# A decoder with ternary weights on one core: the sums of the weights' magnitudes go to ScalarE, and gate and up are rounded one stage earlier and kept in memory

## The chip, the cores and the metric

The kernel runs on one NeuronCore of a Trainium2 chip. Five engines work side by side, each through its own queue of instructions in order: TensorE (PE in the profile, its weight loads PEld), VectorE (DVE), ScalarE (ACT), GpSimd (POOL) and SyncE (SP), which here issues nearly all DMA transfers. They wait for each other through semaphores. The metric is device time in microseconds (us) of one execution; a run's time is 1607.21 us in the median of three (1605.46 to 1613.25).

## The reference

A decoder of two layers works on `x` of 4 x 512 x 512 in float32. Each layer has self-attention, cross attention to a context and a feed-forward network, each followed by an addition and a layer norm. The change lies in the weights of layer 0's feed-forward, whose three matrices (gate and up, 2048 x 512, and down, 512 x 2048) are made ternary:

```python
scale = 1.0 / jnp.clip(jnp.mean(jnp.abs(w)), EPS)
wq = jnp.clip(jnp.round(w * scale), -1.0, 1.0) / scale
```

and then used in

```python
gate = bitlinear(x, w_gate)
up = bitlinear(x, w_up)
intermediate = jax.nn.silu(gate) * up
return h_bitlinear(intermediate, w_down)
```

So the mean magnitude of a whole matrix must be known before its first element can be rounded: each matrix is read twice, once for the mean and once for rounding.

## The kernel before

**Tiling.** Everything is cut into tiles of 128 partitions x 512 columns (256 KB in float32). One of the four batches of one phase is a Python generator; the phases are A (self-attention), B (cross attention), C (feed-forward) of layer 0 and D, E, F of layer 1. `lanes` runs two generators at a time in turn, so the end of one batch overlaps the start of the next, and also the end of A3 with the start of B0. Beside them `step` advances background generators once a round, as `BESIDE` lists: `C0` from A1 to A3, and `C` from B0 to B2.

**The background work before.** `l0_ffn_scales` (`C0`, lines 541 to 571) goes over the 16 chunks of each of the three matrices in the order gate, up, down. It loads a chunk into one of four `w` buffers and VectorE sums its magnitudes into one column (`TENSOR_REDUCE`, L556). After 16 chunks VectorE adds up the columns (L564), a one-column matmul adds over the partitions (`tot`, L567), and VectorE makes mean and scale (L569, L570). `l0_ffn_weights` (`C`, lines 573 to 603) loads all 48 chunks again into the same four buffers. VectorE rounds each by two instructions (L585: times the scale plus a magic number, so that the float's own rounding does it; L586: clipping), and ScalarE casts it to bf16 (L594) into half of a tile of the pool `o`, where it stays until the feed-forward uses it. That pool of 69 buffers also holds the operands of the attention phases.

**The attention phases.** In A, TensorE works in float32 split into a high and a low part: `split` lets ScalarE cast the high part (L141) and VectorE or GpSimd subtract for the low part (L144). Queries and keys go PSUM, ScalarE (L338), VectorE (times sine, L347), GpSimd (times cosine, L350; sum, L355), `split`. GpSimd also adds the bias to `x` (L406) and makes the low part of the next batch's input `xTl` (L144). The softmax takes its maximum on VectorE (L396) and its exponential on ScalarE (L398). In B, one step of the inner loop handles a pair of heads and 128 queries: six score matmuls (L524), maxima on VectorE (L472), exponentials on ScalarE (L474), normalizing on GpSimd (L480), eight transposes on TensorE (L246), copies from PSUM on ScalarE and VectorE (L487), and the output matmuls (L496). There are 64 such steps.

**What sets the order.** A scheduler of the framework orders the instructions of each engine at build time by priorities in program order, data dependencies and free buffers. `issue_after` adds a wish to it: an instruction is queued on its engine behind a named one. `self.mark` names the last multiplication by the sine on VectorE, and the sums of L556 are queued behind it. A `Pipe` delays a step by a number of rounds, so that a load has time to land before its consumer is queued.

## Time and profile before

| What | us |
|---|---|
| Median of the runs, and their range | 1607.21 (1605.46 to 1613.25) |
| The profiled execution's own time | 1603.95 |
| Its span, first to last instruction | 1602.1 |
| Self-attention of layer 0, about | 40 to 245 |
| Cross attention of layer 0, about | 242 to 447 |
| First and last sum of magnitudes (L556) | 48.6 and 227.7 |
| First and last rounding (L585, L586) | 229.0 and 408.0 |
| Last cast to bf16 (L594) | 523.2 |

The page says how busy each engine is; a share over the whole span mixes stages with different limits, so the stages are read one by one, as the busy time of each engine in windows of the span. A row of a tile gives the shortest, median and longest duration of its instructions, and when the first and last of them started. A row of waits gives who waited for whom, the total in us, how often, and the longest.

### The profile page before, as it was taken

How to read it: one execution, taken by the hardware profiler on the slowest of the kernel's cores; microseconds unless marked ns; L12 is line 12 of the kernel's file. 1: busy time of each engine (PE TensorE's matmuls, PEld its weight loads, DVE VectorE, ACT ScalarE, POOL GpSimd, SP SyncE). 2: the span in 40 equal slices, each digit the busy share in tenths (PEclk: the TensorE clock that was granted, in tenths of full speed). 3: DMA queues.
4: the chain of work that ended last, by engine and by line, in shares of the span. 5: the costliest groups of instructions: out<-in, count | busy, mean ns of one | idle time of the engine just before them, and what ended most of it. 6: DMA issues, size and time to landing. Idle time of an engine off the chain costs nothing.

```text
span 1602.1 us, 25568 instructions
## 1 busy us (share of the span) xinstructions
PE 1522.8 (95%) x8246; PEld 1094.9 (68%) x8246; DVE 1237.3 (77%) x2676; ACT 1015.7 (63%) x2193; POOL 666.6 (42%) x672
## 2 busy tenths in 40 slices
PE   8999999999999999999999999999998889999995
PEld 6888785444544674477777767777676766787874
DVE  6486589999876788877575665756869899888896
ACT  5333337988778887787796756968633444645552
POOL 6664654555535204422334242343423345334342
PEclk9999999999999999999999999999999999999998
DMA  7053444455125634852523323233444532020101
GB/s 252 29 171 105 130 161 134 135 171 178 54 79 153 214 108 139 273 175 68 142 58 78 80 87 115 64 80 80 159 158 141 181 100 66 10 80 1 54 0 53
DMA packets 127812, 180.76 MB, mean 113 GB/s; under 512 B 16560, under 2 KB 51376, under 8 KB 127680
## 3 DMA queue, kind: packets, MB, share of 16 engines
q1 hardware_dynamic: 123552, 170.69, 33.9%
q0 software_dynamic: 4128, 8.46, 2.1%
q8 instruction: 65, 1.06, 0.3%
q14 instruction: 67, 0.55, 0.1%
HBM read 111.98 MB, written 41.94 MB: 96 GB/s over the span
## 4 chain that ended last, share of the span: by engine, by line
PE 59%; DVE 19%; ACT 8%; issue 5%; DMA 4%; POOL 3%; SPq 1%; DVEq 0%; ACTq 0%; POOLq 0%
PE fg L1159 7%; PE facc L1142 5%; PE dT L925 3%; DVE bsm L472 3%; PE dn L739 2%; DVE fg L1115 2%; ACT de L915 2%; PE do L945 2%; PE qk L154 2%; PE qk L153 2%; PE qk L152 2%; PE had L753 2%; PE pu L687 2%; PE bo L496 2%; PE pg L685 2%
## 5 line engine op out<-in xcount | busy, mean ns | idle before, releaser
L1115 DVE SCALAR_TENSOR_TENSOR fg<-fg,gs,fg 128x512 f32<-128x512 f32 x220 | 162.2, 743 | 24.6 <-ACT fg L1107 16.2
L911 DVE CUSTOM_DVE_ANT_0 de<-ds,negm,thr 128x128 f32<-128x128 f32 (+3 forms) x256 | 126.4, 545 | 34.6 <-PE ds L900 28.0
L915 ACT ACTIVATE de<-de,dm 128x128 f32<-128x128 f32 (+3 forms) x256 | 143.1, 563 | 12.4 <-DVE dm L911 11.9
L1159 PE MATMUL fg<-fxh,gu 128*128 128x512 f32 x352 | 141.6, 402 | 6.3 <-DVE fg L1115 3.2
L480 POOL TENSOR_SCALAR be<-be,bsm 128x512 f32<-128x512 f32 x128 | 96.1, 764 | 103.0 <-DVE bsm L478 65.5
L1159 PE MATMUL fg<-fxl,gu 128*128 128x512 f32 x352 | 137.5, 391 | 0.0
L662 POOL TENSOR_TENSOR hl<-g,hh 128x512 fp32r<-128x512 f32 x64 | 83.6, 1313 | 109.4 <-ACT hh L661 90.3
L1119 POOL TENSOR_TENSOR fg<-fg,fg 128x512 f32<-128x512 f32 x44 | 60.9, 1384 | 133.0 <-DVE fg L1115 51.9
L474 ACT ACTIVATE be<-bs,bsm 128x512 f32<-128x512 f32 x128 | 87.3, 690 | 30.9 <-DVE bsm L472 28.9
L842 POOL TENSOR_TENSOR dql<-dqf,dqh 128x512 fp32r<-128x512 f32 x32 | 41.3, 1290 | 155.3 <-ACT dqh L841 121.1
L925 PE MATMUL dT<-ident,de 128*128 128x128 f32 x640 | 89.6, 278 | 7.6 <-ACT de L915 5.8
L1159 PEld LDWEIGHTS fg<-fxh,gu 128*128 128x128 f32 x352 | 66.0, 187 | 34.2 <-DVE fg L1115 13.9
L925 PEld LDWEIGHTS dT<-ident,de 128*128 128x128 f32 x640 | 71.7, 141 | 25.3 <-ACT de L915 13.6
L472 DVE TENSOR_REDUCE bsm<-bs 128x1 f32<-128x512 f32 x128 | 83.3, 671 | 0.0
L496 PE MATMUL bo<-bpT,cT 128*64 128x512 f32 x256 | 76.4, 618 | 2.1 <-ACT bpT L487 1.2
L246 PEld LDWEIGHTS bT<-ident,be 128*128 128x128 f32 x512 | 55.0, 141 | 34.2 <-issue 12.3
L246 PE MATMUL bT<-ident,be 128*128 128x128 f32 x512 | 73.3, 281 | 3.7 <-POOL be L480 2.1
L1159 PEld LDWEIGHTS fg<-fxl,gu 128*128 128x128 f32 x352 | 66.1, 188 | 12.0
L350 POOL TENSOR_TENSOR z<-z,rope_cos 128x512 f32<-128x512 f32 x32 | 46.7, 1473 | 64.8 <-DVE zs L347 57.7
L1107 ACT ACTIVATE fg<-fg,gs 128x512 f32<-128x512 f32 x88 | 60.1, 683 | 20.3 <-PE fg L1159 20.3
L1142 PE MATMUL facc<-p4h,fhh 128*128 128x512 f32 x176 | 69.9, 398 | 3.2 <-ACT fg L1111 1.5
L685 PE MATMUL pg<-qT,tb 128*128 128x512 bf16 x256 | 66.8, 381 | 4.4 <-ACT qT L647 2.8
(342 smaller groups left out, 4644.9 us busy)
## 6 DMA issues: line engine op xcount, KB each, us to landing
x<-x SPq DMA_DIRECT2D x176, 256.0 KB, 3.0
had_scratch<-hw SPq DMA_DIRECT2D x64, 256.0 KB, 2.3
z<-had_scratch SPq DMA_DIRECT2D x64, 256.0 KB, 5.8
stk<-dqh SPq DMA_DIRECT2D x192, 64.0 KB, 2.0
tw<-in_wg_t SPq DMA_DIRECT2D x32, 256.0 KB, 3.6
tw<-in_wu_t SPq DMA_DIRECT2D x32, 256.0 KB, 3.7
tw<-in_wd_t SPq DMA_DIRECT2D x32, 256.0 KB, 2.8
p<-in_gu_p SPq DMA_DIRECT2D x22, 256.0 KB, 2.8
```

What stands on the lines that cost most here:

```text
L246: self.nc.tensor.transpose(pt[:, i * P : (i + 1) * P], srcs[i][:, j * P : (j + 1) * P], self.ident)
L472: nc.vector.tensor_reduce(sm[:, h : h + 1], ps, AX.X, ALU.max, negate=True)
L474: nc.scalar.activation(e, ps, AF.Exp, bias=sm[:, h : h + 1], accum_out=sm[:, 2 + h : 3 + h])
L480: nc.gpsimd.tensor_scalar(es[h][i], es[h][i], sm[:, 4 + h : 5 + h], 1.0, ALU.mult, ALU.mult)
L496: nc.tensor.matmul(po[0][h * 64 : h * 64 + 64, :], cT[j][:, c : c + 64], pTs[h], start=j == 0, stop=j == NT - 1)
L685: nc.tensor.matmul(pg, tern["wg_t"][k, c][:, m], qT[k], start=k == 0, stop=k == NT - 1)
L911: nc.vector.tensor_tensor_reduce(es[i], ps, self.negm[:, 384 - P * i :], -1.0, self.thr[:, i : i + 1], ALU.add, ALU.min, n4[:, i : i + 1])
L915: nc.scalar.activation(es[i], es[i], AF.Exp, bias=n4[:, i : i + 1], scale=-1.0, accum_out=den[:, hh * 4 + i : hh * 4 + i + 1])
L925: nc.tensor.transpose(pt[:, o + (i - j) * P : o + (i - j + 1) * P], es[i][:, j * P : (j + 1) * P], self.ident)
L1115: self.emitted["DVE"] = nc.vector.scalar_tensor_tensor(y[u], ps, s, y[u], ALU.mult, ALU.add)
L1142: nc.tensor.matmul(acc[t], h[l][:, c], self.dn[i][r], start=i == 0 and n == 0, stop=i == 10 and n == 2)
L1159: nc.tensor.matmul(ps, self.gu[i, u][:, g * P : (g + 1) * P], xT[g][n], start=n == 0, stop=n == 1)
```

## The change

ScalarE, not VectorE, sums the magnitudes: an Abs with an accumulated sum, queued behind the last evacuation of queries and keys (`self.turned`, recorded in `evac`). The background generator of the self-attention, now `l0_ffn_ternary`, does two things in each of its 48 rounds: it loads a chunk of the matrix whose mean it is taking, and, from the second matrix on, it loads a chunk of the matrix before it into a buffer of `o` (`tq`), rounds it on VectorE, casts it on ScalarE into half of a bf16 tile (`tb`), and stores each full tile to DRAM (`tern_kept`, 8 tiles of 256 KB for each of gate and up). So gate is rounded while up is summed, and up while down is summed. In the cross attention `l0_ffn_weights` rounds the 16 chunks of down alone and, beside them, loads the 16 kept tiles of gate and up back into `o`, one of each in three rounds.

```diff
+        self.tern_kept = {name: scratch(name + "_kept", (8, P, 512)) for name in self.TERNARY[:2]}
...
-            nc.scalar.activation(z, ps, AF.Identity, bias=..., scale=...)
+            self.turned = nc.scalar.activation(z, ps, AF.Identity, bias=..., scale=...)
...
+    def ternary(self, pipe, name, done):
+        nc = self.nc
+        cur = []
+
+        def quant(n, f):
+            with self.tc.issue_after(self.mark.ins):
+                nc.vector.tensor_scalar(f, f, self.scale[name], MAGIC, ALU.mult, ALU.add)
+            nc.vector.tensor_scalar(f, f, MAGIC + 1.0, MAGIC - 1.0, ALU.min, ALU.max)
+            pipe.later(1, put, n, f)
+
+        def put(n, f):
+            if n % 2 == 0:
+                cur.append(self.o("tb", BF16, 1024))
+            o = cur[0]
+            with self.tc.issue_after(self.turned.ins):
+                nc.scalar.activation(o[:, n % 2 * 512 : n % 2 * 512 + 512], f, AF.Copy, bias=-MAGIC)
+            if n % 2:
+                cur.clear()
+                done(n // 2, o)
+
+        return quant
...
-            def absum(f, n):
-                with self.tc.issue_after(self.mark.ins):
-                    nc.vector.tensor_reduce(part[:, n : n + 1], f, AX.X, ALU.add, apply_absolute_value=True)
+        def absum(f, part, n):
+            with self.tc.issue_after(self.turned.ins):
+                nc.scalar.activation(f, f, AF.Abs, accum_out=part[:, n : n + 1])
+
+        def keep(name, n, o):
+            pipe.later(1, lambda: nc.sync.dma_start(self.tern_kept[name][n], o.bitcast(F32)))
+
+        old = None
+        for new in self.TERNARY:
+            chunks = self.ternary_chunks(new)
+            part = self.c(new + "_abs", [P, len(chunks)])
+            if old:
+                quant = self.ternary(pipe, old, lambda n, o, name=old: keep(name, n, o))
+                todo = self.ternary_chunks(old)
+            for n in range(len(chunks)):
+                pipe.tick()
+                pipe.later(1, absum, self.load(self.w("tw"), chunks[n][2]), part, n)
+                if old:
+                    pipe.later(2, quant, n, self.load(self.o("tq"), todo[n][2]))
+                yield
...
+        order = [(name, n) for c in range(0, 8, 2) for name in self.TERNARY[:2] for n in (c, c + 1)]
+        quant = self.ternary(pipe, "wd_t", lambda n, o: use("wd_t", n, o))
+        for n, (name, m) in enumerate(order):
+            pipe.tick()
+            pipe.later(1, quant, n, self.load(self.w("tw"), self.ternary_chunks("wd_t")[n][2]))
+            yield
+            pipe.tick()
+            o = self.o("tb", BF16, 1024)
+            self.load(o.bitcast(F32), self.tern_kept[name][m])
+            use(name, m, o)
+            yield
             yield
```

More of the change, by code (lines that the diff above doesn't have):

```diff
@@ L337, in evac @@
             z = zs[w, m] = self.t("z")
-            nc.scalar.activation(z, ps, AF.Identity, bias=self.qkb[:, w * NT + m : w * NT + m + 1], scale=1.0 if w else P ** -0.5)
+            self.turned = nc.scalar.activation(z, ps, AF.Identity, bias=self.qkb[:, w * NT + m : w * NT + m + 1], scale=1.0 if w else P ** -0.5)
             if m % 2:
@@ L539, in ternary_chunks, with l0_ffn_ternary @@
         return [(k, c, w[k * P : (k + 1) * P, c * 512 : (c + 1) * 512]) for c in range(w.shape[1] // 512) for k in range(w.shape[0] // P)]
-    def l0_ffn_scales(self):
+    def ternary(self, pipe, name, done):
[16 more added lines that the diff above has]
+        return quant
+    def l0_ffn_ternary(self):
         nc = self.nc
@@ L549, in l0_ffn_scales @@
         pipe.later(3, nc.vector.tensor_copy, self.had, f[:, 0:P])
-        for name in self.TERNARY:
-            chunks = self.ternary_chunks(name)
-            part = self.c(name + "_abs", [P, len(chunks)])
-            def absum(f, n):
-                with self.tc.issue_after(self.mark.ins):
-                    nc.vector.tensor_reduce(part[:, n : n + 1], f, AX.X, ALU.add, apply_absolute_value=True)
-            for n, (k, c, ap) in enumerate(chunks):
+        def absum(f, part, n):
[11 more added lines that the diff above has]
+            for n in range(len(chunks)):
                 pipe.tick()
-                pipe.later(1, absum, self.load(self.w("tw"), ap), n)
+                pipe.later(1, absum, self.load(self.w("tw"), chunks[n][2]), part, n)
+                if old:
+                    pipe.later(2, quant, n, self.load(self.o("tq"), todo[n][2]))
                 yield
-            yield from pipe.drain()
-            m = self.c(name + "_mean", [P, 4])
+            pipe.tick()
+            m = self.c(new + "_mean", [P, 4])
             nc.vector.tensor_reduce(m[:, 2:3], part, AX.X, ALU.add)
             yield
+            pipe.tick()
             ps = self.pb("tot")
@@ L568, in l0_ffn_scales, with use @@
             yield
+            pipe.tick()
             nc.vector.tensor_scalar(m[:, 0:1], ps[:, 0:1], 1.0 / (len(chunks) * P * 512), 1e-5, ALU.mult, ALU.max)
             nc.vector.reciprocal(m[:, 1:2], m[:, 0:1])
-            self.mean[name], self.scale[name] = m[:, 0:1], m[:, 1:2]
+            self.mean[new], self.scale[new] = m[:, 0:1], m[:, 1:2]
+            old = new
+        yield from pipe.drain()
     def l0_ffn_weights(self):
-        nc = self.nc
         yield from self.bg["C0"]
         pipe = Pipe()
-        order = [("wg_t", x) for x in self.ternary_chunks("wg_t")]
-        up = [("wu_t", x) for x in self.ternary_chunks("wu_t")]
-        order = [e for c in range(4) for e in order[4 * c : 4 * c + 4] + up[4 * c : 4 * c + 4]]
-        order += [("wd_t", x) for x in self.ternary_chunks("wd_t")]
-        cur = []
-        def quant(name, k, c, f):
-            nc.vector.tensor_scalar(f, f, self.scale[name], MAGIC, ALU.mult, ALU.add)
-            nc.vector.tensor_scalar(f, f, MAGIC + 1.0, MAGIC - 1.0, ALU.min, ALU.max)
-            pipe.later(1, put, name, k, c, f)
-        def put(name, k, c, f):
-            if not cur:
-                cur.append(self.o("tb", BF16, 1024))
-            o = cur[0][:, 0:512] if len(cur) == 1 else cur[0][:, 512:1024]
-            cur.append(o)
-            nc.scalar.activation(o, f, AF.Copy, bias=-MAGIC)
-            self.tern[name][k, c] = o
-            if len(cur) == 3:
-                cur.clear()
-        for name, (k, c, ap) in order:
-            pipe.tick()
-            pipe.later(1, quant, name, k, c, self.load(self.w("tw"), ap))
+        def use(name, n, o):
+            for h in range(2):
+                k, c, _ = self.ternary_chunks(name)[2 * n + h]
+                self.tern[name][k, c] = o[:, h * 512 : h * 512 + 512]
+        order = [(name, n) for c in range(0, 8, 2) for name in self.TERNARY[:2] for n in (c, c + 1)]
+        quant = self.ternary(pipe, "wd_t", lambda n, o: use("wd_t", n, o))
+        for n, (name, m) in enumerate(order):
+            pipe.tick()
+            pipe.later(1, quant, n, self.load(self.w("tw"), self.ternary_chunks("wd_t")[n][2]))
+            yield
+            pipe.tick()
+            o = self.o("tb", BF16, 1024)
+            self.load(o.bitcast(F32), self.tern_kept[name][m])
+            use(name, m, o)
+            yield
             yield
@@ L1240, in body @@
             net.l0_attn_weights()
-        net.bg = {("B", 0): net.l0_xattn_ctx(0), "C0": net.l0_ffn_scales(), "C": net.l0_ffn_weights(), "D": net.l1_attn_weights(), "F": net.l1_ffn_weights()}
+        net.bg = {("B", 0): net.l0_xattn_ctx(0), "C0": net.l0_ffn_ternary(), "C": net.l0_ffn_weights(), "D": net.l1_attn_weights(), "F": net.l1_ffn_weights()}
         f = [net.l0_attn, net.l0_xattn, net.l0_ffn, net.l1_attn, net.l1_xattn, net.l1_ffn]
```

## The prediction

> **What bounds the kernel now.** I read the page first, then the busy time of each engine by stage, then single tiles. The span is 1602.1 us; the profiled execution took 1603.95 us, 3.3 us less than the median of the runs shown (1607.21 us).

> ```profile
> PE 1522.8 (95%) x8246; PEld 1094.9 (68%) x8246; DVE 1237.3 (77%) x2676; ACT 1015.7 (63%) x2193; POOL 666.6 (42%) x672
> ```

> TensorE (PE) is busy nearly always, so the question is where it is held up. The change touches two stages: the self-attention of layer 0 (about 40 to 245 us) and its cross attention (about 242 to 447 us). The busy time by stage of the cross attention (columns: window, its length, busy us of PE, PEld, DVE, ACT, POOL with counts, clock, DMA share, GB/s):

> ```profile
> 280.00:320.00 40.00, 38.51 (x220) 19.05 (x216) 38.62 (x87) 36.51 (x91) 22.44 (x28) 1.00 0.43 139
> 320.00:360.00 40.00, 39.05 (x224) 19.71 (x222) 39.51 (x84) 35.63 (x87) 23.28 (x29) 1.00 0.55 171
> 360.00:400.00 40.00, 38.16 (x223) 19.58 (x222) 39.65 (x89) 35.62 (x87) 23.19 (x30) 1.00 0.54 177
> 400.00:440.00 40.00, 39.45 (x239) 20.48 (x238) 35.10 (x79) 31.09 (x79) 20.92 (x29) 1.00 0.16 56
> ```

> VectorE (DVE) is full up to 400 us, and TensorE gets through 220 to 224 matmuls; in the last window, where the rounding of weights runs out at 408 us, it gets through 239. The timeline of TensorE there shows the undisturbed step of the loop, and the row of its score matmuls the whole stage:

> ```profile
> 423.69 0.50 PE L524 MATMUL bs<-kh,qh 64*128 64x512 f32 x2
> 426.62 0.50 PE L524 MATMUL bs<-kh,qh 64*128 64x512 f32 x2
> 429.54 0.49 PE L524 MATMUL bs<-kh,qh 64*128 64x512 f32 x2
> ```

> ```profile
> L524 PE MATMUL bs<-kh,qh x128: 492/494/502, 241.7 to 444.2; 64*128 64x512 f32 x128
> ```

> One step is 2.92 us undisturbed; the 64 steps start between 241.7 and about 444 us, 3.21 us apart on average. 63 x (3.21 - 2.92) = 18.3 us are lost in this stage. Who causes it, from the waits between 262 and 398 us: VectorE, directly and through ScalarE (ACT) and GpSimd (POOL).

> ```profile
> POOL be L480 <- DVE bsm L478: 28.7, 22, 2.2
> ACT be L474 <- DVE bsm L472: 14.0, 22, 1.7
> PEld bo L496 <- DVE bpT L487: 5.2, 10, 1.2
> ```

> The self-attention is the opposite: TensorE is full, VectorE mostly is not, ScalarE is a third busy. Its last part, cut at the hand-over to the cross attention:

> ```profile
> 160.00:200.00 40.00, 38.25 (x168) 30.35 (x167) 21.40 (x34) 13.97 (x27) 25.82 (x20) 1.00 0.41 129
> 200.00:226.00 26.00, 26.00 (x122) 21.60 (x121) 23.46 (x35) 9.65 (x18) 22.23 (x17) 1.00 0.50 167
> 226.00:246.00 20.00, 19.66 (x99) 15.81 (x99) 18.03 (x41) 7.89 (x19) 0.43 (x1) 1.00 0.49 158
> ```

> **The change, part by part.** The rows of the moved work:

> ```profile
> L586 DVE TENSOR_SCALAR tw<-tw x48: 383/416/1374, 230.0 to 408.0; 128x512 f32<-128x512 f32 x48
> L556 DVE TENSOR_REDUCE wd_t_abs<-tw x16: 658/670/687, 195.8 to 227.7; 128x1 f32<-128x512 f32 x16
> L585 DVE TENSOR_SCALAR tw<-tw,wg_t_mean x16: 465/478/910, 229.0 to 333.0; 128x512 f32<-128x512 f32 x16
> ```

> Neighbours overlap by some 80 ns in these rows, so I count by starts: a sum of magnitudes 0.60 us, the pair that rounds one chunk 0.40 + 0.33 = 0.73 us, the cast on ScalarE (median 626 ns) 0.53 us.

> 1. Cross attention, VectorE. Of 48 pairs, 44 ran here; 16 stay. 28 x 0.73 = 20.4 us leave a stage in which VectorE was full. Load left: the window 400 to 440 held 35.1 us, 2.5 us of it rounding, so 32.6 of 40 (82%) without any; one pair in three steps adds 0.24 per 2.92 us (8%). At 90% VectorE no longer paces TensorE; late next is a short burst (normalizing the previous batch). The undisturbed last batch shows what remains: 15 steps took 45.6 us, 1.8 us over the floor. I take 1.5 us a batch, 6 us in all: gain 18.3 - 6 = 12 us. Bounds: 15 (only the four bursts of about 0.85 us remain) and 7 (twice the residue).

> 2. Cross attention, ScalarE and DMA. 44 casts become 16, which frees 15 us (28 x 0.53) of an engine at 36 of 40; it hides behind VectorE and is in the same gain. 44 loads become 16 loads of the down weights plus 16 of kept bf16 pairs, on SP's queue; nobody needs a kept pair before the feed-forward, over 100 us later for most. The last four casts, at 523 us, leave the feed-forward, where TensorE shows no stall next to them: 0 (bounds 0 and -1.5, the one stall of that batch at 556 us).

> 3. Self-attention, ScalarE. 48 Abs with an accumulated sum: nearest row, Square with accumulation at L1172, 622 ns plus a 192 ns read, 0.6 to 0.7 us by starts, so 29 to 34 us; plus 32 casts, 17 us. Some 48 us on an engine with about 70 us of work in 200 us: it reaches 60%, but an evacuation or cast can now stand behind one sum and one cast (1.1 us). The program gains no load of ScalarE's function table.

> 4. Self-attention, VectorE. 48 sums (28.8 us) leave, 32 - 4 more pairs come (20.4 us): less in total. But they behave differently beside GpSimd. The sums' rows stay within 658 to 687 ns though GpSimd ran at the start of 42 of 48. The second rounding instruction has a median of 0.41 us with GpSimd idle at its start, 0.84 with GpSimd running, at most 1.37; the rope multiply on VectorE (L347) reaches 1.81 from 0.68, and GpSimd's own instructions stretch from 1.28 to 1.82.

> That hits the place where TensorE has no slack, the start of the last batch, where GpSimd works without a break (its timeline):

> ```profile
> 165.60 6.21 POOL L406 TENSOR_TENSOR x<-x,bvo 128x512 f32<-128x512 f32 x4
> 171.77 4.99 POOL L144 TENSOR_TENSOR xTl<-xT,xTh 128x512 fp32r<-128x512 f32 x4
> ```

> TensorE waits 2.5 us there (173 to 177 us). In the new order of VectorE seven rounding instructions lie beside this chain where sums lay; at 0.35 us each they push it by 2.5 us, and the late evacuation ahead of it by 1 us: 3.5 us of stall. Bounds: 0 (each slips into a gap) and 6 (a whole 0.8 us each).

> 5. The hand-over. In the new order 6.2 us of rounding for the up weights lie between 226 and 246 us, where 3.5 us lay; VectorE has about 2 us idle in those 20 us. The softmax of the last batch and the first query tiles stand in the same queue, and TensorE's transposes there started 0.05 us after their ScalarE input. I take 2.5 us; bounds 0 and 6.

> 6. DMA and SP's queue. The transfers of these weights in the self-attention rise from 52 to 96 (256 KB each), 16 of them stores, and each store waits for its second cast with the next loads behind it. In the busiest stretch (215 to 225 us) the queue moved 278 GB/s at a DMA share of 0.85; the new average from 104 us on is about 127 transfers in 141 us, 236 GB/s. It fits, with longer landings; the bound above is in the rival. 0 taken. TensorE's order is unchanged but for the three one-column matmuls of the means, each placed up to 11 us earlier, with the sums then 8 us done.

> [...]

> **Sum.** -12 + 3.5 + 2.5 = -6 us: 1598 us for a profiled execution, 1601 us beside the median of 1607.

> **Rivals.**
> - The self-attention swallows everything, as 40% idle engines suggest; the stalls of steps 4 and 5 stay out. -12 to -14 us: 1594 us. For it: total VectorE work there falls by 8 us. Against it: the zero slack at 173 and 239 us.
> - Both ends cancel: steps 4 and 5 at their upper bounds, 12 - 12: 1607 us.
> - Slower: SP's queue becomes the limit of the self-attention. A store of a kept pair waits for ScalarE, the next load of weights for sums waits behind the store, and ScalarE waits in order for that load with TensorE's evacuations behind it. With 16 stores, 1.6 us exposed at each gives 26 us in place of steps 4 and 5, less 12: 1621 us. It decides from 1.3 us a store. Landings of 3 to 6 us speak for it, four load buffers and the shallow load before 200 us against it.

> That the work is not moved is excluded: VectorE's program is 48 instructions shorter, ScalarE's 48 longer, SP's 32 longer.

> **How the numbers follow.** Forecast 0.41 (own range 1596 to 1606), swallowed 0.25, cancelled 0.18, slower 0.16. What a measurement can tell from no change is 0.5%, 8 us. Faster than 1599.2: all but a little of the second case and 0.12 of the first, 0.36. Slower than 1615: 0.15. Between: 0.49. The range runs from the low end of the second case, 1592, to the cancelled case with the spread of the runs, 1612.

> **What would show it.** Right: the steps of the cross attention near 2.95 us, VectorE at about 36 of 40 there, the first score matmul of the cross attention some 6 us later than 241.7, a longer TensorE stall at 173 us, rounding instructions of 0.8 us and more before 226 us. Wrong: ScalarE or VectorE waiting on DMA of weights for more than 10 us before 245 us (slower), or the cross attention starting on time (faster).

## The result and the profile after

The changed kernel takes 1615.86 us (median of 6 runs, 1613.08 to 1618.94) against 1607.01 us before (6 runs): a ratio of 1.005, 95% interval 1.0036 to 1.0064. It is slower by 9 us; forecast was a gain of 6. Its profiled execution took 1617.94 us, 14.0 us more than that of before; 5 us of this are the draw of the two profiled executions.

The first line of the page shows little:

```profile
PE 1526.5 (94%) x8246; PEld 1100.6 (68%) x8246; DVE 1239.8 (77%) x2628; ACT 1046.7 (65%) x2289; POOL 671.4 (42%) x672
```

The row of the score matmuls cuts the loss in two:

```profile
L525 PE MATMUL bs<-kh,qh x128: 492/494/625, 258.7 to 452.3; 64*128 64x512 f32 x128
```

Before, these ran from 241.7 to 444.2 us. The cross attention starts 17.0 us later and takes 193.6 us instead of 202.5, so it gains 8.9 us. Set against each other matmul by matmul, TensorE is 7.4 us late after 185 us, 14.9 after 232, 17 to 18 at the hand-over, 8.3 at the end of the cross attention, 11.3 from 570 us on, and 13.7 at the end.

The busy time of the cross attention, same stretches and columns as before:

```profile
280.00:320.00 40.00, 39.11 (x233) 19.85 (x232) 36.77 (x80) 35.01 (x88) 25.27 (x30) 1.00 0.44 146
320.00:360.00 40.00, 39.39 (x243) 20.74 (x242) 34.46 (x73) 33.33 (x84) 23.90 (x30) 1.00 0.45 145
360.00:400.00 40.00, 38.93 (x227) 19.58 (x226) 34.18 (x75) 33.23 (x84) 22.96 (x32) 1.00 0.40 132
400.00:440.00 40.00, 40.00 (x250) 21.08 (x246) 32.88 (x72) 33.85 (x86) 22.97 (x31) 1.00 0.28 94
```

VectorE is down from 39 of 40 us to 34 to 37 up to 400 us, and TensorE up to 227 to 250 matmuls. But between 262 and 398 us ScalarE waits longer for VectorE's maxima than the 14.0 us of before:

```profile
ACT be L475 <- DVE bsm L473: 22.7, 28, 2.4
```

The self-attention is where the time went. Stretches of 20 us from 160 us on (window, length, busy us of PE, PEld, DVE, ACT, POOL with counts, granted clock, DMA share, GB/s), and what TensorE waited for between 100 and 262 us, where before it waited only 1.7 us for GpSimd and 0.3 for ScalarE:

```profile
160.00:180.00 20.00, 13.15 (x53) 10.12 (x52) 20.00 (x20) 10.21 (x24) 17.40 (x12) 0.84 0.52 152
180.00:200.00 20.00, 20.00 (x82) 16.33 (x81) 11.09 (x22) 10.19 (x24) 5.78 (x4) 0.90 0.85 285
200.00:220.00 20.00, 20.00 (x97) 16.54 (x97) 19.11 (x22) 12.64 (x28) 13.29 (x9) 1.00 0.52 155
220.00:240.00 20.00, 14.87 (x57) 11.48 (x56) 19.93 (x29) 14.18 (x36) 16.12 (x11) 0.83 0.77 248
```

```profile
PE as L154 <- DVE qkl L145: 6.8, 2, 6.5
PE pv L155 <- DVE apl L145: 3.8, 1, 3.8
PE bs L525 <- ACT qh L468: 2.2, 1, 2.2
PE pv L153 <- ACT aph L142: 1.3, 1, 1.3
```

In the first stretch VectorE is busy for all 20.00 us and gets through 20 instructions, one a microsecond. The timeline at 170 to 178 us shows why (start, us, engine, what, and in brackets what ended the idle time):

```profile
169.79 2.88 POOL L407 TENSOR_TENSOR x<-x,bvo 128x512 f32<-128x512 f32 x2
...
171.48 2.88 DVE L234 TENSOR_SCALAR x<-x,ln 128x512 f32<-128x512 f32 x2
172.63 5.92 POOL L145 TENSOR_TENSOR xTl<-xT,xTh 128x512 fp32r<-128x512 f32 x4
...
174.28 1.48 DVE L550 TENSOR_SCALAR tq<-tq,wg_t_mean 128x512 f32<-128x512 f32 x1
...
175.68 1.75 DVE L145 TENSOR_TENSOR qkl<-z,qkh 128x512 fp32r<-128x512 f32 x1
...
177.35 1.49 DVE L551 TENSOR_SCALAR tq<-tq 128x512 f32<-128x512 f32 x1
...
177.48 0.80 PE L154 MATMUL as<-qkl,qkh 128*128 128x512 f32 x1 [6.48 <-DVE qkl L145]
```

VectorE and GpSimd take turns. Each rounding instruction and each normalization (x<-x,ln, 0.54 us when alone) takes 1.4 to 1.5 us, one GpSimd instruction each (1.44 to 1.48 us here), and the split qkl, which TensorE needs for its scores, is behind them in VectorE's queue. Over the stage this is the row of the second rounding instruction, 0.42 us when GpSimd is idle:

```profile
L551 DVE TENSOR_SCALAR tq<-tq x32: 415/902/1517, 128.4 to 259.4; 128x512 f32<-128x512 f32 x32
```

The 64 rounding instructions before 262 us take 55.2 us of VectorE (28.6 + 14.1 + 12.5 in its groups) instead of 29 (32 x 0.42 + 32 x 0.48).

Then the clock. Stretches of 2 us around the first stall:

```profile
170.00:172.00 2.00, 1.00 (x5) 0.50 (x3) 2.00 (x4) 1.59 (x4) 2.00 (x2) 1.00 0.43 153
172.00:174.00 2.00, 0.00 (x0) 0.00 (x0) 2.00 (x2) 0.00 (x0) 2.00 (x2) 0.91 0.84 213
174.00:176.00 2.00, 0.00 (x0) 0.00 (x0) 2.00 (x3) 0.62 (x1) 2.00 (x3) 0.50 0.79 295
...
180.00:182.00 2.00, 2.00 (x6) 1.52 (x5) 1.33 (x5) 2.00 (x7) 0.00 (x0) 0.50 1.04 394
182.00:184.00 2.00, 2.00 (x6) 1.54 (x6) 1.54 (x3) 1.69 (x4) 0.00 (x0) 0.53 0.66 246
184.00:186.00 2.00, 2.00 (x11) 1.65 (x10) 1.60 (x4) 1.11 (x4) 0.00 (x0) 1.00 0.86 157
```

TensorE stands still from 171.0 to 177.5 us; its granted clock falls to 0.50 at 173.6 and returns at 183.9. In the 6.4 us from its restart to there it does 6 matmuls in 2 us instead of 11, another 3.2 us lost. The first stall so costs 6.5 + 0.4 + 3.2 = 10.1 us where before 2.9 were lost at a full clock (1.7 of them waiting): 7.2 more. The second, at 222 to 232 us, costs 1.3 + 3.8 of waiting and 2.0 of half clock; with small change 7.5. The hand-over adds 2 to 3. In the feed-forward, at 563 us, one wait of TensorE went from 1.3 us (put down to ScalarE) to 2.5 us (put down to a transfer), and a half-clock stretch of 3.4 us followed: 2.9 us more.

### The profile page after: what moved, and what is told of

It reads as the page before. It is cut to its first block, busy times and chain, and to the rows that moved or that the text cites. A ratio compares the mean times of both kernels' runs of the same rounds, so it can differ in the third digit from the quotient of the medians.

```text
span 1616.1 us, 25727 instructions
## 1 busy us (share of the span) xinstructions
PE 1526.5 (94%) x8246; PEld 1100.6 (68%) x8246; DVE 1239.8 (77%) x2628; ACT 1046.7 (65%) x2289; POOL 671.4 (42%) x672
## 4 chain that ended last, share of the span: by engine, by line
PE 61%; DVE 18%; ACT 8%; issue 5%; DMA 5%; POOL 2%; SPq 1%; DVEq 0%; ACTq 0%; POOLq 0%
PE fg L1190 7%; PE facc L1173 5%; PE bo L497 3%; PE bT L247 3%; PE dT L956 3%; PE bs L525 3%; PE dn L770 2%; ACT de L946 2%; DVE fg L1146 2%; PE do L976 2%; PE pg L716 2%; PE dq L153 2%; DVE x L234 2%; PE pu L718 2%; PE dq L154 2%
## 5 line engine op out<-in xcount | busy, mean ns | idle before, releaser
L942 DVE CUSTOM_DVE_ANT_0 de<-ds,negm,thr 128x128 f32<-128x128 f32 (+3 forms) x256 | 126.3, 545 | 34.3 <-PE ds L931 31.2
L946 ACT ACTIVATE de<-de,dm 128x128 f32<-128x128 f32 (+3 forms) x256 | 143.1, 563 | 12.7 <-DVE dm L942 11.3
L1190 PEld LDWEIGHTS fg<-fxh,gu 128*128 128x128 f32 x352 | 66.0, 188 | 34.6 <-DVE fg L1146 13.8
L956 PEld LDWEIGHTS dT<-ident,de 128*128 128x128 f32 x640 | 71.7, 141 | 25.5 <-ACT de L946 13.8
L497 PE MATMUL bo<-bpT,cT 128*64 128x512 f32 x256 | 71.5, 618 | 1.1 <-DVE bpT L488 0.6
```

The lines of the kernel that those rows point to most:

```text
L497: nc.tensor.matmul(po[0][h * 64 : h * 64 + 64, :], cT[j][:, c : c + 64], pTs[h], start=j == 0, stop=j == NT - 1)
L942: nc.vector.tensor_tensor_reduce(es[i], ps, self.negm[:, 384 - P * i :], -1.0, self.thr[:, i : i + 1], ALU.add, ALU.min, n4[:, i : i + 1])
L946: nc.scalar.activation(es[i], es[i], AF.Exp, bias=n4[:, i : i + 1], scale=-1.0, accum_out=den[:, hh * 4 + i : hh * 4 + i + 1])
L956: nc.tensor.transpose(pt[:, o + (i - j) * P : o + (i - j + 1) * P], es[i][:, j * P : (j + 1) * P], self.ident)
L1190: nc.tensor.matmul(ps, self.gu[i, u][:, g * P : (g + 1) * P], xT[g][n], start=n == 0, stop=n == 1)
```

## The experiments

Theory "turns": the rounding, once it runs on VectorE beside GpSimd's instructions, waits a turn for each, and VectorE is late with the splits that TensorE needs. Rivals: SP's queue (loads held up by the stores of kept weights); ScalarE's sums (evacuations behind them); VectorE or the stage simply too full. All runs at a glance (first score matmul, and length of the cross attention from its row):

| kernel | median us | ratio to before, 95% | first score | stage |
|---|---|---|---|---|
| before | 1607.0 to 1608.6 | | 241.7 | 202.5 |
| changed | 1615.86 | 1.005 (1.0036 to 1.0064) | 258.7 | 193.6 |
| e1, form with accumulator | 1614.15 | 1.004 (1.0027 to 1.0053) | 250.5 | 198.5 |
| e2, sums alone | 1609.82 | 1.0014 (1.0002 to 1.0026) | 242.9 | 203.8 |
| e3, rounding alone | 1621.36 | 1.0085 (1.0067 to 1.0103) | 260.6 | 193.3 |
| e4, stores from ScalarE | 1622.96 | 1.0096 (1.0071 to 1.0122) | 263.1 | 194.1 |
| f1, ScalarE rounds gate, up | 1607.89 | 0.9998 (0.9985 to 1.0011) | 246.3 | 194.7 |
| f1c, ScalarE rounds all | 1604.49 | 0.9977 (0.9964 to 0.999) | 246.8 | 191.7 |
| f2, f1 with sums on VectorE | 1613.15 | 1.0035 (1.0023 to 1.0047) | 254.0 | 194.0 |
| g3, f1c begun earlier | 1600.67 | 0.9956 (0.9941 to 0.9972) | 247.4 | 189.4 |
| h1, changed, begun earlier | 1625.41 | 1.0114 (1.0096 to 1.0132) | 267.3 | 191.7 |
| g7, g3 with every fifth step left out | 1603.42 | 0.9971 (0.9959 to 0.9983) | 246.9 | 189.7 |

### e1: the same rounding instructions in a form that also writes out an accumulator

```diff
-nc.vector.tensor_scalar(f, f, self.scale[name], MAGIC, ALU.mult, ALU.add)
-nc.vector.tensor_scalar(f, f, MAGIC + 1.0, MAGIC - 1.0, ALU.min, ALU.max)
+nc.vector.tensor_scalar(f, f, self.scale[name], MAGIC, ALU.mult, ALU.add, accum_out=self.s("acc", 1))
+nc.vector.tensor_scalar(f, f, MAGIC + 1.0, MAGIC - 1.0, ALU.min, ALU.max, accum_out=self.s("acc", 1))
```

> [...] Theory 'turns' (VectorE's rounding and GpSimd's instructions wait for each other, 1.4 to 1.5 us a turn, so VectorE comes late to the splits that TensorE waits for): a rounding instruction takes 0.6 to 0.75 us whether GpSimd runs or not, though it was 0.42 to 0.48 alone; the stalls at 171 us (6.5 us) and 222 us (5.1 us) shrink to less than 3 us together, the half-clock stretches after them go, the first score matmul of the cross attention comes at 243 to 250 us instead of 258.7, and the time is 1598 to 1607 us. Rivals 'SP queue' and 'ScalarE behind its sums': the rounding costs VectorE some 15 us more and nothing else changes, so 1614 to 1622 us with both stalls in place.

The label's one-port form is only a name for this one: the runs show how long its instructions take, not why. This kernel leaves the rounding itself out; the instructions, their order and operands are those of the changed kernel, but for a read of the accumulator (0.08 us) behind each. The row of the second one, and TensorE's waits from 100 to 256 us:

```profile
L551 DVE TENSOR_SCALAR_CACHE_REDUCE tq<-tq x32: 645/686/689, 128.6 to 251.0; 128x512 f32<-128x512 f32 x32
```

```profile
PE bs L525 <- ACT qh L468: 4.4, 1, 4.4
PE pv L155 <- DVE apl L145: 2.1, 1, 2.1
PE as L154 <- DVE qkl L145: 1.1, 2, 0.7
```

The instruction is 0.69 us at most, never 1.5, though GpSimd runs as before. The waits for VectorE's splits fall from 10.6 us to 3.2 and the first score matmul comes 8.2 us earlier. What was lost at the first place is gone (TensorE is 0.2 us late at 200 us); the second, at 217 us, still costs 4.3 us with a half-clock stretch of 3.4. So the stalls come from the long turns of the rounding, and that speaks against the rival of SP's queue as well: SP waits there as in the changed kernel (35.3 and 30.1 us for ScalarE's casts and sums, where the changed kernel has 36.7 and 33.0), and the loads still come late (ScalarE and VectorE wait 11.5 us for weights before 262 us, 15 in the changed kernel). Both marks were missed by little (less than 3 us of stalls, first score matmul by 250 us), and the expected time by more: a pair now costs 1.6 us, the stage after it 4.9 us more than in the changed kernel (198.5 against 193.6), and a stall of 4.4 us at the hand-over takes the place of the two. The cure costs what it saves.

### e2 and e3: each half of the change alone

e2 puts only the sums on ScalarE, on the kernel before; e3 takes the changed kernel and leaves the sums on VectorE:

```diff
-nc.vector.tensor_reduce(part[:, n : n + 1], f, AX.X, ALU.add, apply_absolute_value=True)
+nc.scalar.activation(f, f, AF.Abs, accum_out=part[:, n : n + 1])
```

> The kernel before with one part of the change: the 48 sums of magnitudes go to ScalarE; the rounding of all three weights stays in the cross attention. [...] Rival 'ScalarE behind its sums' (evacuations and casts that TensorE needs stand behind the sums): the first score matmul comes 5 to 12 us later and the time is 1612 to 1619 us.

> The changed kernel with the other part alone: gate and up are rounded in the self-attention and kept in memory, but the sums stay on VectorE. Theory 'turns': VectorE has the turns of the changed kernel and 29 us of sums besides; the two stalls stay, the first score matmul comes at 257 to 266 us and the time is 1615 to 1626 us. Rival 'ScalarE behind its sums': without the sums on ScalarE the stalls are gone and the time is 1597 to 1605 us.

Sums alone: 1609.82 us (from the theory of turns I had put it at 1603 to 1610), first score matmul at 242.9, stage 1.3 us longer than before. 29 us less work on VectorE earn nothing where TensorE is full, and ScalarE's sums cost 1 to 2 us. Rounding alone: 1621.36 us, first score matmul at 260.6; TensorE waits 8.3 us for VectorE's splits and, new here, 4.9 us for ScalarE's exponentials. Both as the theory of turns had it; ScalarE's sums are not the cause.

### e4: the stores of kept weights from ScalarE's queue

```diff
-pipe.later(1, lambda: nc.sync.dma_start(self.tern_kept[name][n], o.bitcast(F32)))
+pipe.later(1, lambda: nc.scalar.dma_start(self.tern_kept[name][n], o.bitcast(F32)))
```

> The changed kernel with the 16 stores of the kept weights issued from ScalarE's own queue, behind the cast that they wait for, instead of from SP's, where 13 of them waited 36.7 us for ScalarE with the loads of weights behind them. Rival 'SP queue': ScalarE's waits for weights in the self-attention (7.4 us, the longest 4.8) go, both stalls shrink to less than 3 us together, and the time is 1598 to 1608 us. Theory 'turns': the stalls at 171 and 222 us keep 8 us or more of their 11.6 us, and the time is 1611 to 1619 us.

TensorE's waits from 100 to 264 us:

```profile
PE as L154 <- DVE qkl L145: 5.9, 1, 5.9
PE bs L525 <- ACT qh L468: 5.5, 1, 5.5
PE pv L155 <- DVE apl L145: 5.0, 1, 5.0
PE pv L153 <- ACT aph L142: 1.5, 1, 1.5
```

Both stalls for VectorE stay (10.9 us; 10.6 in the changed kernel). By itself this does not clear SP's queue: its waits for the stores are gone, but it waits 63.8 us instead of 33.0 for ScalarE's sums to free load buffers, so the loads come no earlier (ScalarE waits 10.0 us for weights instead of 7.4, which the rival expected to go). It is e1 that clears it, where SP waits as in the changed kernel and the stalls shrink. The run is 7 us slower than the changed kernel, 4 more than expected; most lies at the hand-over, where ScalarE waited 4.6 us in order for VectorE's last rounding with casts behind it. Why that came out worse from this queue was not settled.

### f1, f1c and f2: ScalarE rounds

```diff
-nc.vector.tensor_scalar(f, f, self.scale[name], MAGIC, ALU.mult, ALU.add)
-nc.vector.tensor_scalar(f, f, MAGIC + 1.0, MAGIC - 1.0, ALU.min, ALU.max)
-nc.scalar.activation(o, f, AF.Copy, bias=-MAGIC)
+nc.scalar.activation(f, f, AF.Copy, bias=MAGIC, scale=self.scale[name])
+nc.scalar.activation(o, f, AF.Sign, bias=self.magic)   # self.magic: -MAGIC in each partition
```

The sign of the rounded value is the clamped one. f1 does so for gate and up, f1c for down too, f2 is f1 with the sums on VectorE.

> The changed kernel, but gate and up are rounded by ScalarE alone: one Copy with the scale and the magic number, then Sign of the rest, in place of two instructions on VectorE and a cast. VectorE has nothing of the rounding left in the self-attention, ScalarE 32 instructions more (17 us). Theory 'turns': with no rounding beside GpSimd the stalls at 171 and 222 us go, as they shrank with the one-port form, and so does what that form cost VectorE; the first score matmul comes at 242 to 247 us, the cross attention keeps the 194 us of the changed kernel, and the time is 1596 to 1605 us, below the kernel before. Rival 'ScalarE behind its own work': the added 17 us delay the casts and evacuations instead, the first score matmul comes at 250 us or later and the time is 1608 us or more.

> The same, and the down weights too are rounded by ScalarE alone, in the cross attention. There VectorE goes from about 34.3 to 31 of 40 us and ScalarE from 33.7 to 36. If the 0.1 us a step that the changed kernel still loses there is VectorE's, the stage gains 2 to 5 us on the run beside it: 1592 to 1602 us. If it is ScalarE's, the stage loses 2 to 6 us: 1600 to 1609 us.

> As the first run of this group, with the 48 sums of magnitudes left on VectorE. The sums alone were worth nothing on ScalarE (1609.8 against 1608.6 us), and a sum beside GpSimd keeps its 0.67 us. Theory 'turns': what matters is only that no rounding runs on VectorE beside GpSimd, so this stands within 3 us of the first run: 1597 to 1607 us. Rival 'VectorE is simply too full in the self-attention': the 29 us of sums bring a stall back, the first score matmul comes 5 us or more later than in the first run, and the time is 1605 us or more.

In f1 and f1c the stalls at 171 and 222 us are gone, in f2 1.8 us are left of the first; the waits for splits are 1.2, 1.2 and 3.2 us. The one long stall left is at the hand-over, in f1c:

```profile
PE bs L527 <- ACT qh L470: 5.2, 1, 5.2
```

f1 came out between its two expectations (1607.89): right in place, wrong in that I counted the hand-over as cured too. f1c gains 3.0 us of stage on f1, as one of its two expectations had it, though its time (1604.49) misses the range that went with it. So down's rounding on VectorE seems to cost the cross attention time; but 2.3 of the 3.0 us lie in the first batch, where f1's half-clock stretch at the hand-over is also 3.4 us longer (10.2 against 6.8), and the two were not separated. f2 met its rival's number, 5 us slower than f1, and part of its mechanism: its first score matmul comes 7.7 us later than f1's, 3.2 of which are there at 239 us, after short waits for VectorE's splits; the rest comes at the hand-over, where TensorE waits for ScalarE (7.4 us; 4.6 in f1). So a VectorE with the sums on it costs something too, but without the rounding it brings no stall like the two.

### g3 and h1: the same work begun earlier

```diff
-BESIDE = [("A1", "A3", "C0"),
+BESIDE = [("A0", "A3", "C0"),
```

g3 is f1c so changed, h1 the changed kernel. In both the background work also waits until the first batch has set `self.mark`.

> The run in which ScalarE rounds all three weights, with one thing changed: the loads, sums and rounding beside the self-attention begin with its first batch, some 30 us earlier, instead of its second. Question: what holds the queries of the cross attention back for 5.2 us at the hand-over (241.6 to 246.8 us). Theory 'late loads': in the last 20 us the transfers run at 300 GB/s, an up chunk lands 5 us after its issue, and ScalarE waits for it in order with the casts of values and queries behind; with the weights done earlier the stall falls below 1.5 us, the first score matmul comes at 240.5 to 243.5 us, the stage after it keeps its 192 us and the time is 1592 to 1600 us. Rival 'ScalarE is full by its own instructions': the same instructions delay casts elsewhere, TensorE loses 3 us or more in the self-attention and the time is 1601 to 1608 us.

> [...] Theory 'turns': the 64 rounding instructions meet GpSimd again, in other places; VectorE's instructions of 1.3 us and more remain beside GpSimd, TensorE still waits 4 us or more for splits of VectorE in the self-attention, though the hand-over is free, and the time is 1604 to 1614 us, 7 us or more above the run beside it. Rival 'it was the crowding of loads, not the turns': with the loads spread the stalls for VectorE go below 2 us and the time is within 4 us of the run beside it, 1596 to 1603 us.

ScalarE's waits in the last part of the self-attention, f1c (225 to 248 us):

```profile
ACT tq L553 <- DMA tq<-in_wu_t: 6.3, 3, 2.5
```

In g3 ScalarE waits for no weights there (225 to 250 us), and TensorE's waits from 60 to 268 us no longer have ScalarE's queries (qh) among them, only these (shown are all over 0.5 us):

```profile
PE pv L155 <- ACT aph L144: 1.9, 1, 1.9
PE qk L156 <- POOL xTl L147: 1.1, 4, 0.4
PE as L156 <- DVE qkl L147: 0.9, 2, 0.7
PE ap L249 <- ACT ae L401: 0.7, 1, 0.7
```

So the hand-over was late loads: ScalarE stood in order before an up chunk that had not landed, with the casts of values and queries behind. g3 is the fastest kernel of the study, 0.44% under the kernel before. Its time lies between the two expectations, and it misses the first score matmul that was expected (247.4 instead of 240.5 to 243.5): TensorE now loses 6 us earlier in the self-attention, 4 of them at 97 to 103 us, where ScalarE waits 2.7 us for weights with the casts behind, so part of the rival's case holds. h1 is 24.7 us slower than g3. Both begin at the same time; in h1 VectorE rounds (and ScalarE casts), in g3 ScalarE rounds. TensorE's waits in h1, 60 to 268 us:

```profile
PE as L154 <- DVE qkl L145: 12.2, 2, 8.0
PE pv L155 <- DVE apl L145: 4.2, 1, 4.2
```

Spreading the loads did nothing for these waits; they moved and grew, beyond what the theory had expected (1625.41 us, not 1604 to 1614). The loads were not free of waits by it: ScalarE and VectorE still wait 13.8 us for weights in that stretch. TensorE no longer waits for the queries at the hand-over in h1 either.

### g7: fewer steps

```diff
-if plain.index(first) < n <= plain.index(last) + 1 and hasattr(net, "mark"):
+if plain.index(first) < n <= plain.index(last) + 1 and hasattr(net, "mark") and (key != "C0" or net.steps % 5):
```

> The run with the earlier begin and all rounding on ScalarE, with every fifth step of that background work left out, so that it ends near 225 us instead of 200. There ScalarE waited in order for weights from 98 to 107 us with the casts that TensorE needs behind (a stall of 1.9 us and a half-clock stretch), and two shorter stalls at 128 and 177 us; TensorE lost 6 us before 183 us. Theory 'ScalarE's queue is too dense there': with a fifth less per us these fall to 3 us or less, the first score matmul comes at 242 to 245 us and the time is 1595 to 1600 us. Rival 'it only moves': what is gained at 100 us is lost at the hand-over, where loads then come late again; 1600 to 1606 us.

The rival holds. TensorE loses nothing up to 238 us (it is 0.9 us ahead of the kernel before), and then waits 6.0 us for the queries, with ScalarE waiting 6.1 us for three up chunks. The loss moves to the hand-over and the time is 1603.42 us.

## Why the prediction was wrong

1. Cross attention, VectorE: gain 12 us forecast (7 to 15), 8.9 measured. The mechanism is right. The residue was sized from the undisturbed last batch, 1.5 us a batch; the first three batches lost about 3 each (16 steps in 49 to 50 us against a floor of 46.7), the first of them with 3.4 us at half clock. The maxima are still waited for. What the rounding of down still costs there is read from h1 and g3, which begin at the same time and have no half-clock stretch in this stage: 191.7 us with it on VectorE, 189.4 without (12 of the 16 chunks fall in the stage in both).

2. ScalarE and DMA in that stage, and the casts at 523 us: taken at 0 with a bound of -1.5 from the one stall at 556 us. That stall did not go; it grew by 1.2 us and a half-clock stretch followed: +2.9 us. The same wait has 2.3 us in f1 and 2.4 in h1: in f1 a half-clock stretch follows and 2.7 us are lost at this place, in h1 none does and 1.2 are lost. So some 1.5 us of the term are the clock; that they fall due by where the wait lies among the windows of the last section is my estimate, and for f1 and h1 it was not shown.

3. ScalarE's sums in the self-attention: right in size (e2).

4. Self-attention, VectorE beside GpSimd: this step failed. It was sized at 3.5 us with bounds 0 to 6 and measured 7.2 us at the place it named and 7.5 at one it did not name (the value products at 222 us). So 14.7 us stand against 3.5. Three things were wrong in it. The price of a meeting: 0.35 us an instruction was taken, a whole 0.8 us as the bound; it is 1.0 to 1.1 us (0.42 and 0.48 to 1.48), since each waits for a full GpSimd instruction (1.44 to 1.48 us). The trace of before held this price, read one by one: the seven second rounding instructions that started in the middle of a GpSimd instruction took 0.72 to 1.37 us, and each ended 0.28 or 0.29 us after it. What a meeting costs is what is left of GpSimd's instruction, and beside an unbroken chain that is nearly all of it. The company: the four normalizations and the splits in the same queue take turns as well once VectorE has run late into GpSimd's chain. And the stall's price: the short pauses before left the clock at 1.00 (2.9 us lost in all), and the long one was followed by 10.2 us at half clock.

5. Hand-over: 2.5 forecast, 2 to 3 measured; the number is right. Its cause was named as VectorE's rounding. With the rounding on ScalarE (f1c, g3, g7) it is late loads in an in-order queue; in the changed kernel, where ScalarE waits 5.1 us for VectorE's rounding there and VectorE some 3 us for its loads, the two were not separated, so this hit may be partly luck.

6. SP's queue and DMA: 0 taken. ScalarE and VectorE waited 13 us for weights before 245 us, over the 10 us that I had set as the mark of the slower rival, but e1 shows that the two great stalls do not come from there. The sign came out as in the slower rival, by another mechanism.

The sum: -8.9 + 7.4 + 7.5 + 2.1 + 2.9 = +11.0 (7.4 is the 7.2 of the first stall and 0.2 before it), and some 3 us more in small steps behind, half of them in the second layer, make the 14.0 between the two profiled executions.

Of the signs that were to show the forecast right, VectorE's load in the cross attention came as named (36 of 40 us forecast, 34 to 37 measured) and its steps nearly (3.07 us apart, 2.95 forecast); those of the self-attention came too large: a first score matmul 17.0 us late instead of some 6, a stall of 6.5 us at 171 us, rounding instructions of 1.5 us. Two readings of the trace were off without deciding anything: GpSimd ran at the start of 41 of the 48 sums, not 42, and the 2.5 us at 173 us are 1.7 of waiting and 2.9 lost.

For step 4 the rows of before were the better guide to the price. They had a maximum of 1.37 us beside GpSimd, and I went by instructions that met GpSimd now and then, where the moved ones would meet it without a break. In the changed kernel the rounding took 26 us more of VectorE (55.2 against 29); in e1's form the second instruction took 0.69 us at most.

## What to carry to other kernels

Price an instruction by what runs beside it in the place it moves to, at the row's maximum where the neighbour never pauses (here 1.37 us before, 1.52 after, where the median was 0.42), and count the instructions of its own queue that are pulled into the same turns. Freed time on an engine is worth nothing where another is the bound (e2: 29 us off VectorE, first score matmul 1.2 us later), so look for an engine that has room and showed no such turns: here ScalarE's two instructions, 0.72 us each in the mean of g3's self-attention, did what VectorE's two and a cast did. Work moved to an in-order queue must also have its data there early; a load that lands late holds up everything behind it (f1c: ScalarE waited 6.3 us for three up chunks, and TensorE 5.2 us for the queries).

## What the runs showed of the hardware

VectorE and GpSimd in turns run at one instruction of each per 1.45 us in the changed kernel (170 to 179 us): GpSimd's own 128x512 instruction (x<-x,bvo, xTl) goes from 1.27 or 1.29 us at the shortest to 1.44 or 1.48, VectorE's from 0.42 or 0.48 to 1.48. GpSimd loses a little, VectorE two thirds of its rate.
